# First normalization of a decoder kernel: one batch's statistics on ScalarE, tokens copied out in halves, unit products on TensorE, query weights loaded in halves

## The chip, the cores and the metric

The kernel runs on one core of a Trainium2 chip. A core has TensorE (PE in the profile; its weight loads are PEld), VectorE (DVE), ScalarE (ACT), GpSimd (POOL) and SyncE (SP), which issues most DMAs. Each engine works through its own instructions in order; semaphores hold it where it needs something from another. The metric is device microseconds of one execution; the profile is of one execution, and the times come from others.

## What is computed

The input x has 16 batches of 128 tokens with 512 features, all float32. A decoder layer (self-attention, cross-attention, MLP, each behind a layer norm and with a residual) is followed by a second, gated cross-attention:

```python
ln_out = layernorm(hidden_states, ln1_s, ln1_b)
qkv = ln_out @ w_qkv + b_qkv
q, k, v = jnp.split(qkv, 3, axis=-1)
ctx = merge_heads(attention(split_heads(q), split_heads(k), split_heads(v), ltor_mask))
x = hidden_states + ctx @ w_ao + b_ao
...                                   # cross-attention, MLP, gated cross-attention
```

Only the first two lines, for the first four batches, lie in the part of the kernel that is changed.

## The kernel before

The 16 batches form four groups of four (`GB`), so a group has 512 tokens (`TG`). A stage (self-attention A, cross-attention B, MLP C, gated attention D) goes through its groups A0 to A3 and so on. Every instruction is put out through a helper at line 49 that keeps the program's order on each engine, so nothing is reordered: the order of the calls is the order on the engine. Work that has to wait for another engine is put into two lists by `afterwards` (line 78), and `due` (line 81) puts out what is in them before the jobs of the next step.

**Products.** A projection of a group is not four by four blocks multiplied directly but seven products of quarters instead of eight (Strassen-like): `left_blocks` forms four sums of weight quarters (by POOL), `right_blocks` four sums of token quarters (by VectorE for the first group), and `block_product` (line 383) issues the products in a written-out order, `FIRST_BLOCKS` (line 470): for the query weights 1, 2, then 6, 5, then 7, 4, then 3. Products 1 and 2 take quarters as they are: the first half of the columns of the weights and the first two batches of the tokens. Products 1, 6 and 7 accumulate in one PSUM bank (tag `mm0`); after each of them ScalarE copies the bank out (`copy`, line 390) as two instructions of 128x256, and the next of the three needs that copy done.

**The first group.** `begin` (line 751) normalizes the four batches of A0 with the function `normalize` (line 207): VectorE takes mean and variance with `bn_stats` and `bn_aggr` and adds epsilon, POOL raises to the power -0.5, and the rest is left in the list: while `at_start` is set, VectorE subtracts and multiplies (`rest`, line 217); later ScalarE does, with an offset that VectorE works out first (`rest_by_act`, line 222). After that `transpose_batch` turns the batch with four transposes on TensorE, one for each 128 features, into four PSUM banks, which hold one chunk of features of all four batches each. `transposed_out` (line 305) copies the four banks into the tokens' tile, two by ScalarE and two by VectorE, with scale and bias of the layer norm, which stand in columns of a tile that `turn_vectors` makes by a transpose on TensorE. Between them POOL forms the sums of the query weights, and `following.prepare(0)` (line 778) takes the statistics of the first batch of the next group, A1.

`start` (line 782) then forms the token sums on VectorE and goes through the steps of `FIRST_BLOCKS`, with the statistics of A1's other batches (`prepare` 2, 4, 6), POOL's sums of the key and value weights, and small loads beside them. SP's first loads are in the order: four batches of x0, the query weights (1 MB), two batches of x1, the key weights, two batches of x1, a bias row, the value weights.

Of the kernel before, what the change touches and what calls it, by code (L numbers as in the profile page):

```python
# [10 lines left out]
F32 = mybir.dt.float32  # L11
U8 = mybir.dt.uint8
AF = mybir.ActivationFunctionType
ALU = mybir.AluOpType
AX = mybir.AxisListType

P = 128
# [4 lines left out]
H = 512  # L22
NH = 16
HD = 32
KC = H // P
GB = 4
# [3 lines left out]
EPS = 1e-5  # L30
# [22 lines left out]
def decoder_then_gated_cross_attention(ctx: ExitStack, tc: tile.TileContext, a: dict, out: bass.AP):  # L53
    nc = InOrder(tc)

    cpool = ctx.enter_context(tc.tile_pool(name="const", bufs=1))
    wpool = ctx.enter_context(tc.tile_pool(name="weights", bufs=6))
    work = ctx.enter_context(tc.tile_pool(name="work", bufs=1))
# [7 lines left out]
    def ps(tag, name):  # L66
        if tag == "mm" and in_blocks[0]:
            tag = "pt"
        elif tag == "mm":
            flip[0] = (flip[0] + 1) % 4  # L70
            tag = ("mm0", "pt", "mm1", "pt")[flip[0]]
        return psum.tile([P, 512], F32, tag=tag, name=name, bufs={"sc": 4, "pt": 2}.get(tag, 1))
# [3 lines left out]
    late = {"act": deque(), "dve": deque()}  # L76

    def afterwards(engine, do):
        late[engine].append(do)
# [10 lines left out]
    def load_weight(ap, r0, c0, name):  # L90

        t = wpool.tile([P, KC, H], F32, tag="w", name=name)
        nc.sync.dma_start(out=t, in_=ap[r0 : r0 + H, c0 : c0 + H].rearrange("(k p) n -> p k n", p=P))
        return t
# [7 lines left out]
    ident = cpool.tile([P, P], F32, tag="ident", name="ident")  # L102
    make_identity(nc.core, ident)
    mhalf = cpool.tile([P, GB], F32, tag="mhalf", name="mhalf")
    nc.gpsimd.memset(mhalf, -0.5)

    x = [cpool.tile([P, GB, H], F32, tag=f"x{g}", name=f"x{g}") for g in range(NG)]

    def load_batch(g, b):
        nc.sync.dma_start(out=x[g][:, b, :], in_=a["x"][g * GB + b])  # L110
# [33 lines left out]
    def turn_vectors(n):  # L144
        rows, (cols, _) = rows_of[n], columns[vectors[n][0][0]]
        nrow = rows.shape[0]
        tv = ps("mm", f"tv{n}")
        nc.tensor.transpose(tv[:, 0:nrow], rows, ident[0:nrow, 0:nrow])
        nc.vector.tensor_copy(cols, tv[:, 0:nrow])

    def col(name, c):
        cols, row = columns[name]
        return cols[:, row + c : row + c + 1]

    load_vectors(0, nc.scalar)
    w = {}
    w["sq"] = load_weight(a["L0_xattn_w_qkv"], 0, 0, "w_sq")
    for b in range(2):
        load_batch(1, b)
    w["sk"] = load_weight(a["L0_xattn_w_qkv"], 0, H, "w_sk")  # L160
# [40 lines left out]
    def squares(ap):  # L201
        return ap.rearrange("p (c m j) -> p c m j", c=KC, m=NQ)

    def by_chunk(t):
        return t.rearrange("p m c j -> p c m j")

    def normalize(src, dst, name, then):

        mv = work.tile([P, 2], F32, tag="mv", name=f"mv_{name}", bufs=4)
        st = work.tile([P, 6], F32, tag="st", name=f"st_{name}", bufs=4)  # L210
        nc.vector.bn_stats(st, src)
        nc.vector.bn_aggr(mv, st)
        rstd = work.tile([P, 1], F32, tag="rstd", name=f"rstd_{name}", bufs=4)
        nc.vector.tensor_scalar(rstd, mv[:, 1:2], EPS, None, ALU.add)
        nc.gpsimd.tensor_tensor(rstd, rstd, mhalf[:, 0:1], ALU.pow)

        def rest():
            to, of = (by_chunk(dst), squares(src)) if len(dst.shape) == 4 else (dst, src)
            nc.vector.tensor_scalar(to, of, mv[:, 0:1], rstd, ALU.subtract, ALU.mult)
            then()  # L220

        def rest_by_act():

            off = work.tile([P, 1], F32, tag="off", name=f"off_{name}", bufs=4)
            nc.vector.tensor_scalar(off, mv[:, 0:1], rstd, -1.0, ALU.mult, ALU.mult)
            nc.scalar.activation(by_chunk(dst), squares(src), AF.Identity, bias=off, scale=rstd)
            afterwards("dve", then)

        afterwards("dve", rest if at_start[0] else rest_by_act)

    def ln_tile(name):
        return work.tile([P, GB, NQ, KC, Q], F32, tag="ln", name=f"ln_{name}")

    def act_tile(name, tag="actT"):
        return work.tile([P, KC, TG], F32, tag=tag, name=f"T_{name}", bufs=2 if tag == "enc" else 1)
# [64 lines left out]
    def transpose_batch(tp, src, b):  # L300

        for k in range(KC):
            nc.tensor.transpose(tp[k][:, b * S : (b + 1) * S], src[:, b, k * P : (k + 1) * P], ident)

    def transposed_out(t, tp, scale, bias):
        for k in range(KC):
            if k % 2 == 0:
                nc.scalar.activation(t[:, k, :], tp[k], AF.Identity, bias=col(bias, k), scale=col(scale, k))
            else:
                nc.vector.tensor_scalar(t[:, k, :], tp[k], col(scale, k), col(bias, k), ALU.mult, ALU.add)  # L310

    def project_chunk(t, wt, actT, c, name, bias=None, bias0=0, bank="mm"):

# [22 lines left out]
    HF = TG // 2  # L336
# [8 lines left out]
    def left_blocks(wt, t):  # L345


        (a11, a21), (a12, a22) = halves(wt)
        s3, s2, s4, s1 = (*t, a21)[:4]
        return [a11, a12, s4, a22, s1, s2, s3], [  # L350
            (s3, a11, a21, ALU.subtract), (s1, a21, a22, ALU.add), (s2, s1, a11, ALU.subtract),
            (s4, a12, s2, ALU.subtract),
        ]
# [141 lines left out]
    def blocks_plan(products, blocks):  # L495
        out = {}
        for jobs, steps_ in zip(products, blocks):
            for step, ns in steps_.items():
                out.setdefault(step, []).extend((n not in (1, 6, 7), jobs[n]) for n in ns)
        return [([job for _, job in sorted(jobs, key=lambda j: j[0])], [step] * len(jobs)) for step, jobs in out.items()]  # L500
# [128 lines left out]
    def plan(*timed):  # L629

        out = {}
        for jobs, at_ in timed:
            for job, step in zip(jobs, at_, strict=True):
                out.setdefault(step, []).append(job)
        return out
# [95 lines left out]
    class SelfAttention(Section):  # L731
# [19 lines left out]
        def begin(self, following):  # L751

            ln = work.tile([P, GB, H], F32, tag="ln", name="ln_A0")
            self.lnT = act_tile("A0")
            tp = []
            for b in range(GB + 1):
                if b == 1:
                    turn_vectors(0)
                    tp += [ps("sc", f"tp_A0_{k}") for k in range(KC)]
                left = late["dve"].popleft() if b else None  # L760
                if b < GB:
                    normalize(x[0][:, b, :], ln[:, b, :], f"A0_{b}", lambda b=b: transpose_batch(tp, ln, b))
                if left is not None:
                    left()


            at_ = [wpool.tile([P, GB, 2, HF], F32, tag="w", name=f"sums_{n}") for n in range(2)]
            masks = [work.tile([P, 2, 2, HF], F32, tag="mask", name=f"sums_A{n}", bufs=2) for n in range(2)]
            at_ = [t[:, n] for t in at_ for n in range(GB)] + [masks[1][:, 1]]
            SelfAttention.tokens_at = [masks[0][:, 0], masks[0][:, 1], masks[1][:, 0]]  # L770
            SelfAttention.weights = []
            for n, key in enumerate(("sq", "sk", "sv")):
                sides, todo = left_blocks(w[key], at_[3 * n : 3 * n + 3])
                SelfAttention.weights.append(sides)
                SelfAttention.weight_sums.append(todo)
            for o in SelfAttention.weight_sums[0]:
                nc.gpsimd.tensor_tensor(*o)
            following.prepare(0)
            at_start[0] = False
            transposed_out(self.lnT, tp, "ln1_s", "ln1_b")  # L780

        def start(self, following):

            self.begin(following)
            _, todo = self.tiles()
            for o in todo:
                nc.vector.tensor_tensor(*o)
            key_sums, value_sums = self.weight_sums[1:]
            prepare = [lambda p=p: following.prepare(p) for p in (2, 4, 6, 9)], [0, 1, 2, 5]
            jobs = plan(  # L790
                *blocks_plan(self.products(), FIRST_BLOCKS), prepare,
                ([lambda o=o: nc.gpsimd.tensor_tensor(*o) for o in key_sums], [0, 1, 2, 3]),
                ([lambda o=o: nc.gpsimd.tensor_tensor(*o) for o in value_sums], [4, 5, 6, 6]),
                ([load_small, lambda: mask_terms(ms1, ma1)], [2, 5]),
                ([lambda b=b: load_batch(2, b) for b in range(2)], [3, 5]),
            )
            for p in range(max(jobs) + 1):
                due()
                for job in jobs[p]:
                    job()  # L800
            due()
# [874 lines left out]
```

## Time and profile before

| | |
|---|---|
| three timed runs | 1171.96 us median, 1169.91 to 1174.85 |
| profiled execution, span from first to last instruction | 1167.4 us |
| busy share of TensorE / VectorE / ScalarE / POOL | 97% / 65% / 52% / 60% |
| granted TensorE clock, mean | 1.000 |
| chain that ended last | 83% TensorE, 5% POOL, 5% VectorE, 3% issue, 2% DMA |
| first instruction on x0's first batch | 3.49 us (VectorE, ended by its DMA) |
| first multiplication of a projection | 12.62 us |
| first scores | 39.30 us |

The median of the timed runs is 4.6 us above the span of the profiled execution; the difference is what lies around the first and last instruction, and the spread of executions. The profile has the busy time of each engine, 40 slices of the span, the chain of work that was followed back from the last instruction, groups of instructions by tile, and a timeline: start in us, duration in us, engine, line, operation, output and inputs, shape, count, and in brackets how long the engine stood idle before and what ended it. All the kernel's own instructions have line L49, so they are told apart by tile names: `tp_A` are the transposes, `T_A` the tokens of a group in stage A, `mm_q_A` products with query weights, `sums` sums of weight quarters, `sums_A` sums of token quarters, `ln_A` normalized batches, `rstd_A` the power on POOL.

### The profile page before, as it was taken

Reading aid. Unit: us, or ns where it says so; the run is one execution under the profiler, and the core shown is the slowest. Engines: PE = TensorE matmul, PEld = TensorE weight load, DVE = VectorE, ACT = ScalarE, POOL = GpSimd, SP = SyncE. Lnnn points to the kernel's source line nnn. Section 1 sums busy time; section 2 is a strip of 40 time slices with the busy share of each in tenths; the row PEclk is TensorE's granted clock in tenths of the full one; section 3 lists DMA queues with packets and bytes.
Section 4 is the critical chain, followed back from the end, with each engine's and each line's share of the span. In section 5 each row is a group of like instructions: output and inputs, shape, how many; then the busy total and the mean of one; then the engine's idle time right before and its main releaser. Section 6 shows DMA issues by size and latency. Waiting matters only on the chain.

```text
span 1167.4 us, 21612 instructions
## 1 busy us (share of the span) xinstructions
PE 1129.9 (97%) x7202; PEld 861.9 (74%) x7202; DVE 760.5 (65%) x1509; ACT 607.5 (52%) x2132; POOL 701.9 (60%) x636
## 2 busy tenths in 40 slices
PE   7999999999999999998999999999999998999998
PEld 5877777657575757545788888888888776778775
DVE  7678878797878777876663633543432249888773
ACT  2567667666766766674221332232222247876663
POOL 7698878688868775684333423533441367564973
PEclk9999999999999999999999999999999999999999
DMA  6587969899888879898796686695457728988864
GB/s 229 149 223 214 251 181 225 247 243 255 203 229 204 244 203 255 246 293 250 268 297 213 197 263 200 191 318 206 154 194 251 199 56 218 253 233 240 251 200 159
DMA packets 325118, 259.75 MB, mean 223 GB/s; under 512 B 83528, under 2 KB 280336, under 8 KB 320144
## 3 DMA queue, kind: packets, MB, share of 16 engines
q1 hardware_dynamic: 324968, 258.38, 77.1%
q8 instruction: 57, 0.93, 0.3%
q14 instruction: 53, 0.43, 0.1%
q10 hardware_dynamic: 40, 0.01, 0.0%
HBM read 163.94 MB, written 94.37 MB: 221 GB/s over the span
## 4 chain that ended last, share of the span: by engine, by line
PE 83%; POOL 5%; DVE 5%; issue 3%; DMA 2%; ACT 1%; SPq 1%; ACTq 0%; DVEq 0%; POOLq 0%
PE o L49 16%; PE h L49 16%; PE mo_A L49 5%; PE mo_B L49 5%; PE mm_q_B L49 4%; PE mm_v_B L49 4%; PE mm_k_B L49 4%; PE mm_k_A L49 4%; PE mm_q_A L49 4%; PE mm_k_D L49 3%; PE mm_v_A L49 3%; PE mm_q_D L49 3%; PE mm_v_D L49 3%; PE sc_B L49 2%; PE av_A L49 1%
## 5 line engine op out<-in xcount | busy, mean ns | idle before, releaser
L49 DVE TENSOR_TENSOR h<-h,h 128x512 f32<-128x512 f32 x80 | 54.9, 686 | 113.6 <-PE h L49 113.6
L49 ACT ACTIVATE s_A<-s_A,mn_A 128x128 f32<-128x128 f32 x256 | 99.5, 393 | 51.2 <-issue 37.3
L49 ACT ACTIVATE h<-h 128x512 f32<-128x512 f32 x64 | 40.3, 630 | 160.6 <-DVE h L49 160.6
L49 ACT ACTIVATE s_B<-s_B,mn_B 128x128 f32<-128x128 f32 x256 | 99.5, 393 | 46.1 <-issue 32.0
L49 ACT ACTIVATE s_D<-s_D,mn_D 128x128 f32<-128x128 f32 x256 | 99.4, 391 | 32.0 <-issue 16.2
L49 POOL TENSOR_TENSOR s_D<-s_D,sum_D 128x512 f32<-128x512 f32 x64 | 66.6, 1041 | 66.3 <-DVE sum_D L49 56.2
L49 POOL TENSOR_TENSOR s_B<-s_B,sum_B 128x512 f32<-128x512 f32 x64 | 66.9, 1046 | 48.9 <-DVE sum_B L49 40.8
L49 POOL TENSOR_TENSOR s_A<-s_A,sum_A 128x512 f32<-128x512 f32 x64 | 66.7, 1041 | 36.0 <-DVE sum_A L49 35.0
L49 POOL TENSOR_TENSOR s_A<-s_A,ma 128x512 f32<-128x512 f32 x64 | 81.9, 1279 | 5.3 <-DVE s_A L49 3.7
L49 POOL TENSOR_TENSOR s_B<-s_B,mask 128x512 f32<-128x512 f32 x64 | 81.4, 1272 | 2.1 <-DMA away_B<-s_B 0.4
L49 POOL TENSOR_TENSOR rstd_aD<-rstd_aD,mhalf 128x1 f32<-128x1 f32 x12 | 6.6, 548 | 114.6 <-DVE rstd_aD L49 101.1
L49 POOL TENSOR_TENSOR sh<-h 128x512 f32<-128x512 f32 x32 | 40.7, 1273 | 51.0 <-ACT h L49 43.0
L49 PE MATMUL h<-T_C,t 128*128 128x256 f32 x256 | 60.7, 380 | 1.4 <-DVE h L49 1.4
L49 PE MATMUL h<-sx,t 128*128 128x256 f32 x256 | 60.7, 380 | 1.3 <-POOL sx L49 1.3
L49 PE MATMUL h<-T_C,w 128*128 128x256 f32 x256 | 61.0, 381 | 0.8 <-DVE h L49 0.8
L49 PE MATMUL mo_B<-w_co,mT_B 128*128 128x512 f32 x128 | 59.0, 604 | 2.4 <-ACT mT_B L49 2.4
L49 PE MATMUL o<-w,h 128*128 128x256 f32 x256 | 60.5, 379 | 0.0
L49 PE MATMUL o<-t,sh 128*128 128x256 f32 x256 | 60.5, 379 | 0.0
L49 PE MATMUL o<-t,h 128*128 128x256 f32 x256 | 60.5, 379 | 0.0
L49 PE MATMUL mo_A<-w_ao,mT_A 128*128 128x512 f32 x128 | 59.1, 605 | 0.0
L49 PE MATMUL mm_q_B<-T_B,w_cq 128*128 128x512 f32 x128 | 57.3, 595 | 0.0
L49 DVE STREAM_TRANSPOSE s_D<-s_D 128x512 f32<-128x512 f32 x60 | 42.3, 705 | 21.4 <-POOL s_D L49 21.2
(324 smaller groups left out, 2996.7 us busy)
## 6 DMA issues: line engine op xcount, KB each, us to landing
t<-kept SPq DMA_DIRECT2D x24, 1024.0 KB, 7.7
away_A<-s_A SPq DMA_DIRECT2D x64, 256.0 KB, 2.9
pT_A<-away_A SPq DMA_DIRECT2D x128, 128.0 KB, 2.9
away_B<-s_B SPq DMA_DIRECT2D x64, 256.0 KB, 4.3
pT_B<-away_B SPq DMA_DIRECT2D x128, 128.0 KB, 3.7
away_D<-s_D SPq DMA_DIRECT2D x60, 256.0 KB, 3.9
pT_D<-away_D SPq DMA_DIRECT2D x120, 128.0 KB, 2.9
w<-in_L_xattn_w_dram SPq DMA_DIRECT2D x24, 512.0 KB, 5.4
```

The costliest lines, as they stand in the source:

```text
L49: return lambda *args, **kw: self.tc.keep_in_program_order(call(*args, **kw))
```

## The change

All of it lies before and in the first group's normalization.

- The query weights are loaded by two DMAs, first half of the columns first.
- TensorE multiplies the unit matrix with itself into a bank that nothing reads: eight times at the start, three times after the vectors' transpose, twice after the first batch's transposes.
- Batch 1's statistics are taken by ScalarE and POOL (`normalize_beside`): a sum, its share with the sign turned, a sum of squares, POOL's scaling and power; VectorE still subtracts and multiplies. The order of the batches is 1, 0, 2, then 3.
- The four PSUM banks are copied out for two batches at a time: the first half of the tokens by ScalarE, four instructions of 128x256, the second half by both engines, two each.
- `following.prepare(0)` moves from the middle of `begin` to a place in `start` behind the token sums, and so behind the line that clears `at_start`.

```diff
-    w["sq"] = load_weight(a["L0_xattn_w_qkv"], 0, 0, "w_sq")
+    w["sq"] = wpool.tile([P, KC, H], F32, tag="w", name="w_sq")
+    for half in range(2):
+        nc.sync.dma_start(
+            out=w["sq"][:, :, half * (H // 2) : (half + 1) * (H // 2)],
+            in_=a["L0_xattn_w_qkv"][:, half * (H // 2) : (half + 1) * (H // 2)].rearrange("(k p) n -> p k n", p=P),
+        )
...
+    def normalize_beside(src, dst, name, then):
+
+        col_tile = lambda tag: work.tile([P, 1], F32, tag=tag, name=f"{tag}_{name}", bufs=4)
+        total, off, rstd = col_tile("total"), col_tile("off"), col_tile("rstd")
+        nc.scalar.activation(dst, src, AF.Identity, accum_out=total)
+        nc.scalar.mul(off, total, -1.0 / H)
+        nc.scalar.activation(dst, src, AF.Square, bias=off, accum_out=total)
+        nc.gpsimd.tensor_scalar(rstd, total, 1.0 / H, EPS, ALU.mult, ALU.add)
+        nc.gpsimd.tensor_tensor(rstd, rstd, mhalf[:, 0:1], ALU.pow)
+
+        def rest():
+            nc.vector.tensor_scalar(dst, src, off, rstd, ALU.add, ALU.mult)
+            then()
+
+        return rest
...
-            tp = []
-            for b in range(GB + 1):
-                if b == 1:
-                    turn_vectors(0)
-                    tp += [ps("sc", f"tp_A0_{k}") for k in range(KC)]
-                left = late["dve"].popleft() if b else None
-                if b < GB:
-                    normalize(x[0][:, b, :], ln[:, b, :], f"A0_{b}", lambda b=b: transpose_batch(tp, ln, b))
-                if left is not None:
-                    left()
+            warm = ps("mm", "warm")
+
+            def keep_going(n):
+                for _ in range(n):
+                    nc.tensor.matmul(warm[:, 0:P], ident, ident, start=True, stop=True)
+
+            tp = [ps("sc", f"tp_A0_{k}") for k in range(KC)]
+            rest = {}
+
+            def statistics(b):
+                args = x[0][:, b, :], ln[:, b, :], f"A0_{b}", lambda b=b: transpose_batch(tp, ln, b)
+                if b == 1:
+                    rest[b] = normalize_beside(*args)
+                else:
+                    normalize(*args)
+                    rest[b] = late["dve"].pop()
+
+            def turned_half(half, by_act):
+                t = slice(half * HF, (half + 1) * HF)
+                for k in range(KC):
+                    if k in by_act:
+                        nc.scalar.activation(
+                            self.lnT[:, k, t], tp[k][:, t], AF.Identity, bias=col("ln1_b", k), scale=col("ln1_s", k)
+                        )
+                    else:
+                        nc.vector.tensor_scalar(
+                            self.lnT[:, k, t], tp[k][:, t], col("ln1_s", k), col("ln1_b", k), ALU.mult, ALU.add
+                        )
+
+            keep_going(8)
+            for b in (1, 0, 2):
+                statistics(b)
+            turn_vectors(0)
+            keep_going(3)
+            rest[0]()
+            keep_going(2)
+            statistics(3)
+            rest[1]()
+            turned_half(0, range(KC))
+            rest[2]()
+            rest[3]()
+            turned_half(1, (1, 3))
...
-            following.prepare(0)
             at_start[0] = False
-            transposed_out(self.lnT, tp, "ln1_s", "ln1_b")
...
             _, todo = self.tiles()
             for o in todo:
                 nc.vector.tensor_tensor(*o)
+            following.prepare(0)
```

More of the change, by code (lines that the diff above doesn't have):

```diff
@@ L303, in transpose_batch @@
             nc.tensor.transpose(tp[k][:, b * S : (b + 1) * S], src[:, b, k * P : (k + 1) * P], ident)
[L305 to L310, printed above, removed]
     def project_chunk(t, wt, actT, c, name, bias=None, bias0=0, bank="mm"):
```

## The prediction

> **What bounds the kernel now.** I read the page first: TensorE is busy 97% of a span of 1167.4 us, and the chain that ended last is 83% TensorE. So the kernel is one long row of multiplications, and a change at the beginning is worth what it moves the point from which TensorE runs without a gap. Then the timeline of the first 45 us, by engine:
>
> ```profile
> 9.74 1.48 DVE L49 TENSOR_SCALAR ln_A<-x,mv_A,rstd_A 128x512 f32<-128x512 f32 x1 [0.44 <-POOL rstd_A L49]
> ...
> 11.28 1.11 PE L49 MATMUL tp_A<-ident,ln_A 128*128 128x128 f32 x4 [0.80 <-DVE ln_A L49]
> 11.79 1.45 ACT L49 ACTIVATE T_A<-tp_A,vcols 128x512 f32<-128x512 f32 x2 [8.53 <-PE tp_A L49]
> ...
> 12.62 5.76 PE L49 MATMUL mm_q_A<-T_A,w_sq 128*128 128x256 f32 x16 [0.23 <-ACT T_A L49]
> ...
> 16.44 0.84 ACT L49 ACTIVATE q_A<-mm_q_A,vcols 128x256 f32<-128x256 f32 x2 [3.20 <-PE mm_q_A L49]
> ...
> 18.22 1.89 PE L49 MATMUL mm_q_A<-sums_A,sums 128*128 128x256 f32 x8
> ```
>
> Columns: start, duration, engine. The last normalization (9.74) leads to the last transposes (11.28), the copies out of PSUM (11.79) and the first multiplications (12.62). From there TensorE has no gap of note until 39.3. The first 16 rows (query products 1 and 2; a multiplication of the program is two rows) take 18.22 - 12.62 = 5.60 us, 0.35 each; the next 8 take 1.72, 0.215 each. In small windows the rows start 0.427 apart until about 16.6, then 0.216. So about ten rows run at half speed: 10 x 0.21 = **2.1 us**. The granted clock reads 1.00 all the while, so this column does not show it.
>
> One more place matters, product 7 of the query weights:
>
> ```profile
> 20.25 0.81 ACT L49 ACTIVATE ln_A<-x,off_A,rstd_A 128x512 f32<-128x512 f32 x1 [2.97 <-DVE off_A L49]
> ...
> 20.97 0.82 ACT L49 ACTIVATE q_A<-mm_q_A,vcols 128x256 f32<-128x256 f32 x2
> ...
> 21.84 0.51 PEld L49 LDWEIGHTS mm_q_A<-T_A,sums 128*128 128x128 f32 x3 [0.41 <-ACT q_A L49]
> ```
>
> Products 1, 6 and 7 share one PSUM bank. A product of these may start only when ScalarE has copied the one before out of the bank, and here those copies stood behind a normalization of the next group on ScalarE. TensorE lost 0.41 us. From the start of that normalization to TensorE's release it is 21.84 - 20.25 = 1.59 us.
>
> **The change, part by part.** *Query weights in halves.* One more DMA on SP, 0.43 us as the whole one took; all behind it (x1, key weights, bias row, value weights) is issued that much later. The engines move 373 to 419 GB/s over most of 12.6 to 17 us and fall to nothing at 18, so the queue is never short of work. 1 KB packets take 46 ns against 84 for 2 KB: 64 x 46 - 32 x 84 = 0.26 us more per engine. First needs behind it are x1 at about 17 us and key weights at about 20. Cost 0, bounds 0 and 0.4. The first half comes earlier, but the first product waits for the transposes, so that gains nothing.
>
> *Thirteen multiplications of the unit matrix.* The first eight start at about 1.4 us, when the matrix is made; TensorE idles until 4.44 and again until 6.43. Their 16 rows have no like: a 128-column transpose row takes 0.213, a cold 256-column row 0.427, so they end between 4.8 and 8.2; nearest is the weight load of a cold row, 0.333, so about 6.7. The transposed vectors wait behind them, and on VectorE the copy of these stands ahead of batch 0's normalization, which (next part) can't start before 7.6. Cost 0, at worst 0.6 for the chain below.
>
> *Batch 1's statistics.* ScalarE now does sum (128x512, 0.63 as the gelu of this size), mean (0.20), squares (0.71), each sum with a reading of the accumulator (0.19, half of it overlapped). Semaphores put batch 1's landing at 4.12: 4.15 + 0.8 + 0.2 + 0.8 gives 6.0. POOL then scales (no like: 0.29, the affine select, to 0.79, the slower power; I take 0.4, near the select) and raises to the power (0.56), 7.0. **Batch 0's power stands behind these two on POOL**, though its input is ready at 4.6: 7.6, where it was done at 5.3. So batch 0's normalization moves from 5.84 to 7.7. Then, by the distances of the timeline: batch 3's statistics 8.15, batch 1's normalization 9.15 and batch 2's 9.6, both without a statistics row between, batch 3's power done 9.9 to 10.1 (before: 9.71), its normalization 1.48 beside POOL's first weight sum as before, so 11.4 to 11.6 (before: 11.22). The second and fourth batch are no earlier.
>
> *Halves of the tokens.* ScalarE copies the first half: four of 128x256, 0.42 apart as for q_A, about 10.2 to 12.0. The order of instructions shows batch 2's transposes wait, chunk by chunk, for these copies (same banks), so batch 2's end at 12.2 and batch 3's run 12.2 to 13.3. The first product is queued behind: **13.1, against 12.62**. The second half is copied by 13.7 on both engines (before: 13.67), and VectorE's four token sums end 2.5 to 3.5 us after 13.5, so 16.0 to 17.0 (before: 17.14; one of the four took 1.57 beside POOL).
>
> *The next group's first batch is moved* behind the token sums. Its statistics were taken at 11.14, its power was waiting in POOL from 15.35, and VectorE normalized it. Now statistics follow the token sums: 1.1 us (3.49 to 4.59 for batch 0), power 0.6, offset 0.25, and since the start flag is off by then, **ScalarE normalizes it, and that instruction stands ahead of the copy of product 1** in ScalarE's order. Product 6 waits for that copy. So: 16.0 to 17.0, + 1.1 + 0.6 + 0.25 + 1.59 (the row above) = 19.5 to 20.5, with POOL's scaling at its slow end up to 20.9. Before, it was 18.22. Added wait 1.3 to 2.7; I take 20.3, **+2.1 us**, since one slow token sum is as likely as before.
>
> *What the faster clock saves is covered by this wait*: products 1 and 2 end at 13.1 + 3.45 = 16.5 warm or 18.7 cold, and either way product 6 starts at 20.3. Behind product 6, SP's sends of the group, POOL's key sums and the mask loads shift by the same 2 us. Before, the third key sum was done at 26.07 for a product at 28.85; now POOL's order (power, sum, bias row, power, sum, bias row, power, sum) from 20.0 gives 27.9 for a product at about 30.8, so no new wait.
>
> Sum: -0 (clock) + 2.1 (product 6) + 0 (loads) = span 1169.5. The three timed runs have a median 4.6 above the profiled span; that stays, so **1174.0**.
>
> [...] Here transposes filled 4.46 of the 6.20 us before 12.6, and the first ten rows were still slow, while a gap of 2.48 us at 967 cost no speed. [...]
>
> **The rivals.** (a) *The wait does not bind, and the change does what it says*: product 6 starts as product 2 ends. It decides if ScalarE's normalization ends by 15.7, so that the copy is out by 16.5, which is 3.8 earlier than in the forecast. Price: 16.5 - 18.22 = -1.7, 1170.2. For it: the order leaves ScalarE idle before; against: five steps in a row, each with a row. This one ends on the faster side. (b) *The clock falls back during the wait*: rows from product 6 on start 0.427 apart again, ten rows, +2.1 more: 1176.1. For it: 3.8 us is longer than any gap of this trace; against: gaps up to 2.48 cost nothing. (c) *The unit matrix does not warm the clock*: products 1 and 2 end at 18.7, the wait is 1.6 and costs the same: 1174 again. (d) *POOL's key sums come late.* The third has 30.8 - 27.9 = 2.9 us to spare; it decides when POOL loses more than that, and a bias row of 1.27 beyond it would be the price: 1175.3. For it: POOL is busy 11.25 of the 11.8 us after 18.2; against: nothing in the order adds work to it there.
>
> **How the numbers follow.** The forecast, with (c) in it: 0.66; (a) 0.13; (b) 0.16; (d) 0.05. The three runs of before lie 1169.9 to 1174.9, so each case has some 2.5 to both sides. The range of 8 in 10 reaches from (a) to (b): 1169.8 to 1177.6. A difference under 0.5% (5.9 us) is about what a measurement of this kernel can tell from no change; no case alone passes it: faster 0.03, same 0.88, slower 0.09.
>
> **What would show it.** In the changed profile: product 6 (mm_q from token sums) at about 20.3 with an idle time of 1.6 to 4 us ended by ScalarE's q_A copy; that copy right behind a ScalarE normalization ln_A; batch 0's power done at about 7.6; the first products at about 13 and 0.216 apart (warm) or 0.427 (c); after the wait 0.216 (forecast) or 0.427 (b). The forecast is wrong if product 6 starts before 18.2, or if TensorE has a second long wait before 42.

## The result, and the profile after

| | before | after |
|---|---|---|
| median of 7 runs each | 1172.83 us | 1176.82 us (1174.28 to 1179.24) |
| ratio of the times | | 1.0039, interval 1.0024 to 1.0054 |
| span of the profiled execution | 1167.4 us | 1173.5 us (its own time 1175.54) |
| mean granted clock in it | 1.000 | 0.993 |
| product 6 of the query weights starts | 18.22 us | 21.39 us |
| first scores | 39.30 us | 43.96 us |

The changed kernel is slower by 4.0 us, nearly twice the forecast's 2.1; its time is inside the forecast's range. The timeline of its beginning (start, duration, engine, operation, count; idle time before it, and what ended it, in brackets):

```profile
1.34 3.79 PE L49 MATMUL warm<-ident 128*128 128x128 f32 x16 [1.34 <-POOL mhalf L49]
...
9.94 1.93 ACT L49 ACTIVATE T_A<-tp_A,vcols 128x256 f32<-128x256 f32 x4 [3.93 <-PE tp_A L49]
...
10.56 2.17 PE L49 MATMUL tp_A<-ident,ln_A 128*128 128x128 f32 x8 [0.33 <-ACT T_A L49]
...
12.53 5.30 PE L49 MATMUL mm_q_A<-T_A,w_sq 128*128 128x256 f32 x16
13.13 1.27 POOL L49 TENSOR_TENSOR sums<-w_sq 128x512 f32<-128x512 f32 x1
13.39 1.56 DVE L49 TENSOR_TENSOR sums_A<-T_A 128x512 f32<-128x512 f32 x1
14.48 1.59 POOL L49 TENSOR_TENSOR sums<-w_sq,sums 128x512 f32<-128x512 f32 x1
15.06 1.57 DVE L49 TENSOR_TENSOR sums_A<-T_A,sums_A 128x512 f32<-128x512 f32 x1
...
17.15 0.68 DVE L49 TENSOR_TENSOR sums_A<-sums_A,T_A 128x512 f32<-128x512 f32 x1
17.75 0.68 DVE L49 BATCH_NORM_STATS2 st_A<-x 128x6 f32<-128x512 f32 x1
...
19.75 0.81 ACT L49 ACTIVATE ln_A<-x,off_A,rstd_A 128x512 f32<-128x512 f32 x1 [6.22 <-DVE off_A L49]
...
20.47 0.82 ACT L49 ACTIVATE q_A<-mm_q_A,vcols 128x256 f32<-128x256 f32 x2
...
21.39 2.41 PE L49 MATMUL mm_q_A<-sums_A,sums 128*128 128x256 f32 x8 [3.55 <-POOL rstd_A L49]
...
23.59 3.17 PE L49 MATMUL mm_q_A<-sums_A,w_sq 128*128 128x256 f32 x8
```

From the bottom up: product 6 (21.39) stands 3.55 us still. The profile puts this down to a power on POOL, which is the event nearest in time; in the program, product 6 waits for ScalarE's copy of product 1 (20.47, done at 21.29) and for a weight sum of POOL's that was done long before. That copy stands behind the normalization at 19.75, for which ScalarE had stood idle 6.22 us; its statistics (17.75) follow the last token sum (17.15). Two of the token sums took 1.56 and 1.57 us; before, one did.

The same stretch in windows (busy us and count of PE, PEld, DVE, ACT, POOL; then the granted clock, the DMA share and GB/s):

```profile
13.00:16.00 3.00, 3.00 (x9) 2.38 (x8) 2.90 (x4) 0.53 (x2) 2.84 (x3) 0.51 1.05 385
16.00:18.00 2.00, 1.83 (x9) 1.28 (x7) 2.00 (x4) 0.00 (x0) 0.08 (x1) 1.00 0.71 263
18.00:20.00 2.00, 0.00 (x0) 0.00 (x0) 1.27 (x5) 0.25 (x1) 0.55 (x1) 1.00 0.04 14
...
22.00:24.00 2.00, 2.00 (x8) 1.64 (x7) 1.69 (x6) 0.98 (x2) 2.00 (x3) 0.69 0.44 131
24.00:26.00 2.00, 2.00 (x6) 1.60 (x5) 1.58 (x5) 1.41 (x3) 2.00 (x3) 0.50 0.61 164
26.00:30.00 4.00, 4.00 (x19) 3.47 (x19) 0.79 (x2) 0.84 (x2) 4.00 (x5) 0.98 0.44 131
```

The clock column reads about a half twice: in the first products (the trace's clock records: 12.5 to 15.9) and after the wait (22.8 to 26.2). Six rows in the two microseconds from 24 to 26 are about half of the eleven that a clock of 1.00 gives there (experiment 12).

Matching the instructions of the two profiled executions, after lies 4.66 us behind from 40 to 480 us, 5.1 to 5.2 from 540 to 1120 and 6.2 at the end. So 3.17 is product 6's wait and 1.49 the stretch behind it. The last 0.5 and 1.0 belong to half-clock stretches at 531 to 538 and 1132 to 1136, at places where TensorE waits in both kernels; the profiled execution of before had none of them.

### The profile page after: what moved, and what is told of

Read it like the earlier page. It is cut to its first block, busy times and chain, and to the rows that moved or that the text cites. A ratio compares the mean times of both kernels' runs of the same rounds, so it can differ in the third digit from the quotient of the medians.

```text
span 1173.5 us, 21678 instructions
## 1 busy us (share of the span) xinstructions
PE 1138.4 (97%) x7228; PEld 868.5 (74%) x7228; DVE 757.9 (65%) x1506; ACT 611.8 (52%) x2142; POOL 701.1 (60%) x637
## 4 chain that ended last, share of the span: by engine, by line
PE 86%; DVE 4%; POOL 3%; issue 2%; DMA 2%; ACT 2%; SPq 1%; DVEq 0%; POOLq 0%; ACTq 0%
PE o L49 16%; PE h L49 16%; PE mo_A L49 5%; PE mo_B L49 5%; PE mm_q_B L49 4%; PE mm_v_B L49 4%; PE mm_k_B L49 4%; PE mm_v_D L49 4%; PE mm_k_D L49 4%; PE mm_k_A L49 3%; PE mm_v_A L49 3%; PE mm_o_D L49 3%; PE mm_q_D L49 3%; PE mm_q_A L49 3%; PE sc_B L49 2%
## 5 line engine op out<-in xcount | busy, mean ns | idle before, releaser
L49 PE MATMUL mo_B<-w_co,mT_B 128*128 128x512 f32 x128 | 61.8, 628 | 3.1 <-ACT mT_B L49 3.1
L49 DVE STREAM_TRANSPOSE s_D<-s_D 128x512 f32<-128x512 f32 x60 | 42.3, 705 | 21.5 <-POOL s_D L49 21.2
```

The source lines that it names most:

```text
L49: return lambda *args, **kw: self.tc.keep_in_program_order(call(*args, **kw))
```

## The experiments

Theory: the moved statistics put a ScalarE normalization ahead of the copy of product 1, and the wait behind that costs first itself and then a stretch of half clock. Rivals: the halves, the unit products or ScalarE's statistics cost the time; or the clock falls there by itself. "Shift" is the first scores against 39.30 us in the profiled execution of before.

**1. Flag later.** The move stays, but the start flag is cleared behind it, so that VectorE normalizes A1's first batch.

```diff
-            at_start[0] = False
...
             following.prepare(0)
+            at_start[0] = False
```

> The changed kernel with one line moved: the start flag is cleared behind the statistics of A1's first batch, so that VectorE normalizes this batch (as before the change) and nothing stands ahead of the copy of product 1 on ScalarE. Theory (ScalarE's order): product 6 starts when product 2 ends, at 17.7 instead of 21.4, TensorE has no wait there, its rows behind it stay 0.216 apart, the first scores come at 38.7 to 39.3 (changed kernel 43.96, before 39.30) and the time is 0 to 1 us under that of before, some 4.5 under the changed kernel's. Rival (the token sums on VectorE come too late, whoever normalizes): product 6 at 20 or later, the time of the changed kernel within 1 us.

Measured 1176.68 us, ratio 1.0024 [1.0010, 1.0037], shift +2.20. Product 6 starts at 18.95, with no gap behind product 2: what held it in the changed kernel was ScalarE's order. That it came 1.2 later than expected is slow rows, in spite of the unit products: the first batch's four transposes take 1.12 us in this execution (0.66 in the changed kernel), twelve more 3.77, and the 16 rows of products 1 and 2, from 13.45, 5.67. But the time did not come back; the timeline of this kernel:

```profile
22.45 0.81 ACT L49 ACTIVATE ln_A<-x,off_A,rstd_A 128x512 f32<-128x512 f32 x1 [4.51 <-DVE off_A L49]
...
23.17 0.81 ACT L49 ACTIVATE q_A<-mm_q_A,vcols 128x256 f32<-128x256 f32 x2
...
24.04 1.99 PE L49 MATMUL mm_q_A<-T_A,sums 128*128 128x256 f32 x8 [1.48 <-ACT q_A L49]
```

The same thing one product later: product 7 waits for the copy of product 6, and this stands behind the normalization of A1's second batch. Here the profile names ScalarE's copy itself.

**2. Statistics back ahead of the token sums**, everything else as changed. In the kernel before they also stood ahead of VectorE's copies out of PSUM; here they stand behind these.

```diff
             for o in SelfAttention.weight_sums[0]:
                 nc.gpsimd.tensor_tensor(*o)
+            following.prepare(0)
             at_start[0] = False
...
-            following.prepare(0)
```

> The changed kernel with the statistics of A1's first batch put back to their old place, ahead of the token sums on VectorE and with the flag still set. Theory (ScalarE's order): the copy of product 1 is out at 17, but the statistics' 1.1 us now stand ahead of the token sums, so the second sum is done at 17.7 and product 6 starts at 17.8 to 18.3; first scores 38.9 to 39.5, time within 1 us of before. Rival (late token sums): they come 1.1 later still, product 6 at 21 or later and the time no better than the changed kernel's.

Measured 1174.58 us, ratio 1.0006 [0.9992, 1.0020], shift +1.15. Product 6 starts at 17.72, before its time in the old kernel, and product 7 waits 1.65 us (0.41 before). With the statistics there, the kernel is half a microsecond ahead of the old one at product 6 and 1.14 behind it at product 7 (22.98 against 21.84).

**3. The move alone**, in the kernel before.

```diff
-            following.prepare(0)
             at_start[0] = False
             transposed_out(self.lnT, tp, "ln1_s", "ln1_b")
...
             for o in todo:
                 nc.vector.tensor_tensor(*o)
+            following.prepare(0)
```

> The kernel before with only this part of the change: the statistics of A1's first batch moved behind the token sums and the flag's clearing. Theory (ScalarE's order): token sums end at 17.1, statistics 1.1, power 0.6, offset 0.25, then 1.6 for normalization and copy: product 6 at 20.3 to 20.8 instead of 18.22, first scores +2.1 to +2.6, and up to 1.7 more if the clock falls in the wait; time 1175 to 1177 where before has 1173. Rival (it takes ScalarE's statistics, the halves or the unit products): product 6 at 18.2 and the time of before.

Measured 1175.95 us, ratio 1.0024 [1.0009, 1.0040], shift +4.19. Its timeline:

```profile
19.28 0.81 ACT L49 ACTIVATE ln_A<-x,off_A,rstd_A 128x512 f32<-128x512 f32 x1 [7.07 <-issue]
...
20.00 0.82 ACT L49 ACTIVATE q_A<-mm_q_A,vcols 128x256 f32<-128x256 f32 x2
...
20.92 3.25 PE L49 MATMUL mm_q_A<-sums_A,sums 128*128 128x256 f32 x8 [4.13 <-POOL rstd_A L49]
```

The three lines of the changed kernel again, with half clock behind them (0.57 from 21 to 25 us). One moved line makes nearly the whole difference; that 4.19 and the 1.15 of experiment 2 are more than 4.66 shows that the two losses overlap.

**4. No unit products**, everything else as changed.

```diff
-            keep_going(8)
...
-            keep_going(3)
...
-            keep_going(2)
```

> The changed kernel without the thirteen products of the unit matrix. Theory: they are worth nothing, since product 6 waits for ScalarE: product 6 at 21.0 to 21.4, products 1 and 2 slow for about ten rows and done at 18.1, a wait of 3.3. The time is the changed kernel's within 1.7 us; lower by about 1.5 if the shorter wait leaves the clock up behind product 6. Rival (the unit products save what the clock costs at the beginning): 2 us slower than the changed kernel.

Measured 1175.12 us, ratio 1.0019 [1.0003, 1.0035]. Product 6 starts at 21.36 behind a wait of 3.21; its eight rows take 2.41 us and the next eight 3.18, as in the changed kernel (2.41 and 3.17). The shift is +4.64 against +4.66 with the unit products: here they are worth nothing, the wait covers them.

**5. Into a gap of VectorE's**, ahead of the second half's copies, the flag still set.

```diff
             rest[3]()
+            following.prepare(0)
             turned_half(1, (1, 3))
...
-            following.prepare(0)
```

> The changed kernel with the statistics of A1's first batch ahead of the second copies, where VectorE waits for the last transposes (flag still set, so VectorE normalizes). Theory (with ScalarE's order mended, VectorE's row of work is the bound: token sums, statistics of A1's second batch, offset, then ScalarE's normalization and copy, then product 7): the second batch's statistics start at 18.3 as before the change (19.42 with the statistics behind the copies), product 7 at 21.8 to 22.0, first scores 39.2 to 39.6, time within 1 us of before. Rival (the halved copies, which hold the transposes, cost the 1.15 us that were left): first scores 40.2 or later.

Measured 1176.83 us, ratio 1.0032 [1.0019, 1.0045], shift +2.23: a miss. In the timeline:

```profile
11.76 0.55 POOL L49 TENSOR_TENSOR rstd_A<-rstd_A,mhalf 128x1 f32<-128x1 f32 x1 [1.83 <-DVE rstd_A L49]
...
12.27 1.27 POOL L49 TENSOR_TENSOR sums<-w_sq 128x512 f32<-128x512 f32 x1
...
22.47 0.81 ACT L49 ACTIVATE ln_A<-x,off_A,rstd_A 128x512 f32<-128x512 f32 x1 [5.50 <-DVE off_A L49]
...
24.07 1.99 PE L49 MATMUL mm_q_A<-T_A,sums 128*128 128x256 f32 x8 [2.78 <-ACT q_A L49]
```

The power of the moved statistics now stands ahead of POOL's weight sums. These start at 12.27 instead of 10.25 and fall beside the token sums, three of which take 1.57 to 1.75 us; VectorE is late with the statistics of A1's second batch, and product 7 pays for it. A DVE instruction was moved into a gap, and its follower on POOL was forgotten.

**6. The other statistics a step later**, on top of 5, so that ScalarE copies products 6 and 7 first.

```diff
-            prepare = [lambda p=p: following.prepare(p) for p in (2, 4, 6, 9)], [0, 1, 2, 5]
+            prepare = [lambda p=p: following.prepare(p) for p in (2, 4, 6, 9)], [1, 2, 3, 5]
```

> The kernel with the statistics in the gap, and the statistics of A1's other three batches one step later, so that ScalarE's copy of product 6 no longer stands behind a normalization that waits for VectorE. Theory: product 7 follows product 5 without a wait, 3.5 us behind product 6; with product 6 at 17.5 to 18 the first scores come at 38.4 to 39.0 and the time is 0.3 to 0.9 us under before. Rival (the work only moves: A1's batches, sent later, are waited for in the next steps): first scores earlier, but the time is that of before or above, with a new TensorE wait between 40 and 100 us.

Measured 1173.09 us, ratio 1.0003 [0.9991, 1.0015], shift -0.32. Product 6 starts at 18.16 and product 7 at 21.62, neither with a wait: with ScalarE's normalization out of the way of the copy, the loss is gone. That the time is 0.3 to 0.9 us under before, as expected, can't be told from this ratio.

**7. First half's copies behind all transposes**, on both engines, on top of 6.

```diff
-            turned_half(0, range(KC))
...
             following.prepare(0)
+            turned_half(0, (1, 3))
             turned_half(1, (1, 3))
```

> As the one before, and the copies of the first half put behind all transposes, on both engines, so that the third batch's transposes no longer wait for ScalarE. Theory: transposes end at 11.3 instead of 12.4, first product at 11.8 to 12.2, product 6 at 16.8 to 17.6, first scores 37.9 to 38.5, time 0.8 to 1.5 us under before. Rival (VectorE's token sums end no earlier): product 6 at 17.7, time as the kernel before it.

Measured 1173.07 us, ratio 1.0004 [0.9989, 1.0018], shift -0.18: a miss, at least 0.8 was expected. The transposes no longer wait for the copies; the products start at 12.69, 16 rows in 3.72 us, and product 6, ready at 16.4, waits 1.11 us, to 17.52, for POOL's weight sums. The bound has gone to POOL.

**8. Unit products between the transposes**, on top of 7.

```diff
+            keep_going(3)
             rest[2]()
+            keep_going(3)
             rest[3]()
+            keep_going(4)
```

> As the one before, with ten more unit products between the transposes, so that TensorE multiplies in every stretch from 1.4 to 12 us. Theory (transposes and a few products are too little to hold the clock): the first products run at 0.216 from the start, products 1 and 2 end at 15.5 to 16, product 6 waits for the second token sum to 16 to 16.8, first scores 36.8 to 37.6, time 1.5 to 2.5 us under before. [...]

Measured 1172.62 us, ratio 0.9998 [0.9987, 1.0009], shift -0.01: a miss, 1.7 to 2.5 were expected. The 16 rows from 13.22 take 3.62 us, where in the changed kernel, at half clock from 12.5, they took 5.30; but product 6 waits 0.85 us for POOL all the same.

**9. POOL's weight sums first**: ahead of the statistics, on top of 8. **10. The same without any unit product.**

```diff
             keep_going(4)
+            at_ = [wpool.tile([P, GB, 2, HF], F32, tag="w", name=f"sums_{n}") for n in range(2)]
...
+            for o in SelfAttention.weight_sums[0]:
+                nc.gpsimd.tensor_tensor(*o)
             following.prepare(0)
             turned_half(0, (1, 3))
             turned_half(1, (1, 3))
-            at_ = [wpool.tile([P, GB, 2, HF], F32, tag="w", name=f"sums_{n}") for n in range(2)]
...
```

> The version before this one, with POOL's three sums of query weights put out ahead of the statistics of A1's first batch, so that the power for that batch stands behind them on POOL. There product 6 came at 17.69 after 0.85 us of waiting for POOL's sums. Theory (POOL's and VectorE's chain in front of product 6 is all that is left): the wait goes, product 6 starts at 16.8 to 17.1, the first scores at 38.4 to 38.7 against 39.30 in the kernel before, and the time is 0.6 to 0.9 us under that of the kernel before, ratio 0.9993. Rival (it is the token sums on VectorE, slowed beside POOL): product 6 at 17.5 to 18.2 with a wait that token sums end, scores at 39.2 or later, ratio 1.000 or above.

> The same kernel without any product of the unit matrix. Theory: now that nothing else holds product 6, the cold rows are on the path: the first projections start at about 13 us, rows 0.427 apart for ten to sixteen rows, products 1 and 2 end at 18.2 to 19, product 6 there, scores at 39.4 to 40.3, 1 to 1.6 us later than with the unit products. Rival (the unit products are worth nothing here either): scores within 0.3 us of the kernel with them.

Measured 1172.33 us, ratio 0.9987 [0.9975, 0.9998], shift -1.61 for the first; 1172.48 us, 0.9987 [0.9973, 1.0000], shift -0.46 for the second. Product 6 of 9 came as expected; its scores came 0.7 earlier than expected, since a wait of 0.42 for a copy at 25.29, which 8 had besides, went too. The timeline of 9:

```profile
13.13 3.62 PE L49 MATMUL mm_q_A<-T_A,w_sq 128*128 128x256 f32 x16
16.80 1.96 PE L49 MATMUL mm_q_A<-sums_A,sums 128*128 128x256 f32 x8
18.61 1.89 PE L49 MATMUL mm_q_A<-sums_A,w_sq 128*128 128x256 f32 x8
```

The same place in 10:

```profile
13.42 4.77 PE L49 MATMUL mm_q_A<-T_A,w_sq 128*128 128x256 f32 x16 [0.34 <-DVE T_A L49]
18.03 1.89 PE L49 MATMUL mm_q_A<-sums_A,sums 128*128 128x256 f32 x8
```

Behind the first product no line of 9 has a bracket: TensorE has no gap from there on. With nothing else in the way the unit products are worth 16 rows in 3.62 instead of 4.77 us: 37.69 against 38.84 at the first scores, 1.15 us (1 to 1.6 were expected), while in experiment 4 they were worth nothing. This is read from one execution of each; the medians, 1172.33 and 1172.48, don't show it.

**11. The later steps alone**, in the kernel before: the one line of experiment 6.

```diff
-            prepare = [lambda p=p: following.prepare(p) for p in (2, 4, 6, 9)], [0, 1, 2, 5]
+            prepare = [lambda p=p: following.prepare(p) for p in (2, 4, 6, 9)], [1, 2, 3, 5]
```

> The kernel before with one edit: the statistics of A1's other batches at the steps 1, 2, 3, 5 instead of 0, 1, 2, 5. Theory: ScalarE's normalization of A1's second batch no longer stands ahead of the copy of product 6, so the 0.41 us that product 7 waited goes: scores at 38.9 against 39.30, ratio 0.9997. Rival (the wait moves to the next copy): scores at 39.3 or later.

Measured 1171.41 us, ratio 0.9985 [0.9971, 0.9998], shift -0.10. From product 6 to the scores it is 20.81 us instead of 21.08, without the wait of 0.41, but product 6 came 0.17 later (18.39), so that 0.10 is left at the scores. Its ratio is that of experiment 9, whose beginning is 1.5 us shorter: the times of kernels this near to each other do not rank them. The profiles do, for the beginning.

**12. The wait filled**: fourteen more unit products between products 2 and 6 of the changed kernel, into a bank that nothing reads.

```diff
             for p in range(max(jobs) + 1):
                 due()
+                if p == 1:
+                    spare = ps("sc", "spare")
+                    for _ in range(14):
+                        nc.tensor.matmul(spare[:, 0:P], ident, ident, start=True, stop=True)
```

> The changed kernel with fourteen more products of the unit matrix (28 rows of 0.107 us, 3.0 us) put out between products 2 and 6 of the query weights, into a bank that nothing reads, so that TensorE works through most of the 3.55 us in which it waited for ScalarE's copy. Nothing else is changed, and nothing later starts earlier. Theory (the wait itself costs 3.17 us, and the clock that falls because of it another 1.49): product 6 still starts at 21.3 to 21.5, but the rows behind it are 0.216 us apart, no stretch of half the clock lies at 22.8 to 26.2, and the first scores come at 42.3 to 42.7, 3.0 to 3.3 us later than in the kernel before instead of 4.66. Rival (the clock falls there for another reason): half the clock behind product 6 as before, scores at 43.8 to 44.1.

Measured 1174.71 us, ratio 1.0013 [1.0002, 1.0025] where the changed kernel has 1.0039; shift +2.56. Its timeline:

```profile
17.82 3.29 PE L49 MATMUL spare<-ident 128*128 128x128 f32 x28
...
20.97 1.96 PE L49 MATMUL mm_q_A<-sums_A,sums 128*128 128x256 f32 x8
...
22.77 1.89 PE L49 MATMUL mm_q_A<-sums_A,w_sq 128*128 128x256 f32 x8
```

Its windows, with the columns as above:

```profile
22.00:24.00 2.00, 2.00 (x11) 1.77 (x10) 1.33 (x5) 1.41 (x3) 2.00 (x4) 1.00 0.44 121
24.00:26.00 2.00, 2.00 (x11) 1.75 (x10) 1.71 (x5) 0.81 (x1) 2.00 (x2) 1.00 0.65 171
```

TensorE does useless work in the wait, and what follows is faster: eleven rows in each two microseconds instead of eight and six, the clock at 1.00. From product 6 to the first scores it is 41.86 - 20.97 = 20.89 us, against 43.96 - 21.39 = 22.57: the falling clock cost 1.68, near half of the 3.41 us that the stretch lasts. That the scores came a little before the expected 42.3 is product 6, which started 0.42 earlier because the token sums ended 0.42 earlier.

## Why the prediction was right, and where its size was off

- *The bound, and what a change at the beginning is worth*: right. The shift at 40 us is the shift at 480 us.
- *Halves, unit products and ScalarE's statistics at nothing*: right as far as the runs can tell (4.64 against 4.66 without the unit products; 2, without the move: the interval of its ratio takes in 1, while its profile is 1.15 behind; the move alone gives 4.19 of the 4.66). Powers and normalizations came within 0.2 of their forecast times up to batch 2: batch 0 normalized at 7.49 (forecast 7.7), batch 1 at 8.98 (9.15). Batch 3's was done at 10.60 instead of 11.4 to 11.6, since POOL's first weight sum, beside which it was to be slow, waited for its weights until 10.25; in 1 and 12, without that wait, it was done at 11.47 and 11.51. The unit rows ended at 5.13 instead of 6.7, POOL's scaling took 0.19 instead of 0.4, the first product came at 12.53 instead of 13.1: all on the early side, and nothing of it reached product 6.
- *The moved statistics*: right mechanism and place (3). From the end of the token sums to product 6 the forecast had 1.1 + 0.6 + 0.25 + 1.59 = 3.54; it was 21.39 - 17.83 = 3.56.
- *The term that was mis-sized*: "token sums end 16.0 to 17.0", with "one slow token sum as likely as before". They ended at 17.15 + 0.68 = 17.83. The 2.5 to 3.5 us that it gave the four sums leave out before's own 3.55 (13.59 to 17.14). It let them follow VectorE's copies, but their end follows POOL. POOL's timeline of before, with its last two weight sums:

```profile
12.43 1.26 POOL L49 TENSOR_TENSOR sums<-w_sq 128x512 f32<-128x512 f32 x1
13.77 1.62 POOL L49 TENSOR_TENSOR sums<-w_sq,sums 128x512 f32<-128x512 f32 x1
```

And VectorE's, with the first two token sums and the last:

```profile
13.59 0.68 DVE L49 TENSOR_TENSOR sums_A<-T_A 128x512 f32<-128x512 f32 x1
14.37 1.57 DVE L49 TENSOR_TENSOR sums_A<-T_A,sums_A 128x512 f32<-128x512 f32 x1
...
16.46 0.68 DVE L49 TENSOR_TENSOR sums_A<-sums_A,T_A 128x512 f32<-128x512 f32 x1
```

In before, VectorE's first sum (13.59) starts as a POOL sum ends (13.69) and takes 0.68; the next POOL sum, begun inside it, takes 1.62 instead of 1.26, and VectorE's second sum, begun inside that, takes 1.57. After, POOL's sums are 0.70 later, 0.23 of it a wait for the weights, and VectorE's first sum 0.20 earlier, so it starts inside a POOL sum. It ends at 13.39 + 1.56 = 14.95, 0.55 behind that POOL sum's end (13.13 + 1.27 = 14.40), and the second ends at 16.63, 0.56 behind the end of the next (14.48 + 1.59 = 16.07). In before the slow one ends at 14.37 + 1.57 = 15.94, 0.55 behind POOL's 13.77 + 1.62 = 15.39. So in both profiles a slow token sum ends 0.55 or 0.56 us behind the POOL sum beside it, and 0.68 is what a sum takes that starts after them. What holds it there was not shown.

So the token sums end here 1.75 us behind POOL's last weight sum, whether one of them is slow or two: 15.39 and 17.14 in before, 16.07 and 17.83 after. Experiment 12 is the changed program up to this place; its POOL sums did not wait for the weights, and only one token sum was slow:

```profile
14.06 1.60 POOL L49 TENSOR_TENSOR sums<-w_sq,sums 128x512 f32<-128x512 f32 x1
...
16.73 0.68 DVE L49 TENSOR_TENSOR sums_A<-sums_A,T_A 128x512 f32<-128x512 f32 x1
```

These end at 15.66 and 17.41, 1.75 apart again, and product 6 starts at 20.97. So of the step's 1.07 above the forecast 2.1, some 0.65 lie in the program's order and 0.42 in that one execution, where POOL began 0.28 later and its first sum took 1.47 instead of 1.27. The first part could have been forecast: the forecast's batch 3 power at 10.0, four POOL sums as in before (9.68 to 15.39, 5.71 us), 1.75 and 3.54 make 21.0, an estimate from rows of before. The wait for the weights is not shown to come from their halves: 3, which loads them whole, has it too (0.58 us), and 1 and 12 don't.

- *"What the faster clock saves is covered by this wait"*: right, and shown from both sides: unit products are worth 0.02 with the wait (4) and 1.15 without it (9 against 10). The warm-up itself failed besides, as in rival (c): the changed kernel's clock records begin with 1.00 at 5.7, and fall to a half at 12.5, behind a stretch with little but transposes. With unit products between these, the 16 rows of products 1 and 2 took 3.62 us (8, 9) instead of 5.30. How much of that is their doing is open, since executions with the same eight unit products at the start differ before that place: four transposes at 8.1 took 0.66 us in the changed kernel and 1.12 in 1, and the four weight loads of the transposes at 9.6 took 0.42 us in the changed kernel and 0.71 in 6.
- *The clock after the wait*: the forecast went by "a gap of 2.48 us at 967 cost no speed", rival (b) by the falling clock. Rival (b), given 0.16, is what happened, on top of the forecast's wait and at 1.68 instead of 2.1 (12); the range held the time because it had been drawn out to (b). A single execution was too little for that step: before's profiled execution has a clock of 1.000, but the mean of 116 others is 0.996; and at the same wait near 970, before (2.48 us) and after (2.50) kept a clock of 1.00, while 9 reads 0.52 from 968 to 975. At the beginning, waits of 1.48, 1.65 and 2.78 us (1, 2, 5) were followed by eight rows in 1.99 us, and waits of 3.21, 3.55 and 4.13 (4, after, 3) by eight rows in 2.41, 2.41 and 3.25. What decides it was not shown (the last section has TensorE's shares in two profiles).
- *POOL's key sums*, rival (d): no; the key product from them started at 33.51 with no gap. Rival (a): product 6 at 16.80 without a wait is what experiment 9 reached, by further moves.

The sum for the profiled beginning is 3.17 (wait) + 1.68 (clock) - 0.19 (product 7's old wait and the like, 20.89 against 21.08 in before) = 4.66. The forecast had the first term at 2.1 and the second at 0.16 odds. How much of the timed 4.0 is either can't be told closer than the scatter of executions.

## What to carry to other kernels

A statistic that is moved takes its whole train along: the power on POOL, the offset, the normalization on whichever engine the flag then selects. Follow each follower to its place in its engine's order, and ask which copy or sum is queued behind it. A gain ahead of a wait is worth nothing until the wait is gone, so remove the last wait first, and then measure the same part again. Where the runs show one engine's work ending behind another's, as VectorE's slow sums ended 0.55 us behind POOL's here, forecast the end of one's work from the other's row. And where a change makes TensorE stand still, count slow rows behind the wait too: here they followed waits of 3.21 to 4.13 us.

## What the runs showed of the hardware that was not expected

- The clock fell behind 3.41 us in which TensorE had worked for 40%. By the clock records of the changed kernel's trace, its half-clock stretches last 3.413 us, or twice that at 531, except the last (2.727, at the end of the records). Cut into pieces of 3.413 us by these records, the piece that ends at 22.76 is one in which TensorE stood still until 21.39, 60% of it, and then worked, and the clock was halved at its end. Cut in this way, the profiles of before and after have 670 pieces at full clock behind 17 us. The five in which TensorE was busy for 0, 4, 31, 38 and 40% were followed by half clock, and none of the other 665, with 42% or more; the waits near 970 have pieces of 54% (before) and 49% (after) at the lowest. (The ends of multiplications are modelled in a profile, so the shares are rough.) Ahead of 17 us it was otherwise: the piece from 9.11 to 12.52, busy for 68%, most of it with transposes, was followed by half clock too.
- Useless multiplications in a wait made the time behind it 1.68 us shorter (12).
- Executions of one kernel differ by up to 7 us (before: 1169.8 to 1176.9 in 35 runs), more than the whole change moves. Half-clock stretches behind 500 us can be a part of that: before's profile has none up to 1167.1, after's has two, of 6.83 us at 531 and 3.41 at 1132, with 0.5 and 1.0 us of shift behind them. How much of the difference they make was not shown.
